# Perceiver layer on one core: the weighted context in four single PSUM banks, with its last sums, the first query products and the down products laid out differently

## The chip, the cores and the metric

The kernel runs on one core of one Trainium2 chip. The metric is device time in microseconds (us) for one execution, lower is better; the figure given is the median of repeated runs. A profile is one further execution recorded by the hardware profiler. All arithmetic is fp32.

A core has five engines that run side by side, each with its own instruction stream: TensorE (PE in the profile; its weight loads appear as PEld), VectorE (DVE), ScalarE (ACT), GpSimd (POOL) and SyncE (SP, which issues most DMA transfers). They hand work to each other through semaphores. TensorE writes its products into PSUM[...].

## The reference

One layer of a Perceiver on 256 tokens x of width 512, with a context c of 25088 rows of width 512:

```python
# 1 cross attention with a sigmoid in place of a softmax
q = layernorm(x) @ Wq.T + bq            # 256 x 128
k = c @ Wk.T + bk                       # 25088 x 128
z = sigmoid(q @ k.T / sqrt(128))        # 256 x 25088
x = x + z @ (c @ Wv.T + bv)
# 2 causal attention: 16 query heads of 64, one shared key and value head
x = x + layernorm(attention(layernorm(layernorm(x))) @ w_out.T)
# 3 experts: a shared one (1024 wide, gated) plus the top 8 of 64 (256 wide each), weighted
h = layernorm(x)
x = x + shared(h) * sigmoid(h @ shared_gate) + sum(w_e * expert_e(h))
```

The kernel uses z @ (c @ Wv.T + bv) = (z @ c) @ Wv.T + rowsum(z) * bv. It keeps two sums over the context: the "weighted context" zc = z @ c (256 x 512) and the "score sums" rowsum(z) (256 values).

## The kernel before, in words

**Context loop (L480-494).** The 25088 rows are taken in 49 groups of 512 (G = 49, four row blocks of 128 each, J = 4). For each group TensorE makes keys (`pk`), scores (`pz`), ScalarE the sigmoid (`zT`), and TensorE adds zT times context to the weighted context (`xacc`). That last product is done by seven block products in place of eight, with sums of blocks made beforehand by VectorE: `query_sums` (S, from zT) and `context_sums` (T, from the context). The seven products (named "00", "01", "2", "3", "1", "4", "11" at L436) are each 128 x 256 and stay in PSUM through all 49 groups. They share banks in pairs: `banks("xacc_0")` and `banks("xacc_1")` are tiles of two banks each. "00" with "01" and "2" with "3" lie in the first tile; "1" with "4", and "11" alone, in the second. VectorE also adds every zT into `zsum` (128 x 4 x 256), from which the score sums come.

**Last sums (L497-546).** After the last group VectorE combines the seven products into zc with eight instructions, TensorE transposes zc in eight blocks (`transposed`, L301), VectorE copies the transposes to zcT, TensorE forms the score sums `pr` from the four parts of zsum, and then py = zcT times Wv for each of the two token tiles (t = 0 and 1). x1, its layernorm `an` and the transposes of an follow.

**Heads (L794-817).** Sixteen heads are handled as eight pairs (NE = 8), which the text calls heads 0 to 7, in a software pipeline. Iteration e transposes the exponentials of head e-2 (`turned`), divides those of head e-1 (`divided`: a reciprocal on VectorE, a product on GpSimd), makes the queries of head e+2 (`queries`: products on TensorE into `pa`, a scaled copy `aq` on VectorE for heads 1 to 3 and on ScalarE for the others), makes the scores of head e (`scored`: products `ps`, mask and maxima on VectorE), the weighted values of head e-2 (`weighted`, `po`), and the exponentials of head e (`exponential`, on ScalarE). When queries run out, parts of the output projection (`fill`, `project`, product `pw`) take their place.

**Experts (L892-1287).** For the shared expert (in four pieces) and eight whole experts: `gate_up` makes `ph` from the tokens and the first weights, ScalarE and VectorE make the hidden values hT, and `down` multiplies them with the second weights for the two token tiles (`pd`), which VectorE weights and adds to `y`. Seven less-used experts are taken in blocks of 32 rows (`few_...`) between them, and `few_spread` adds their result to y.

**Order and buffers.** `in_turn` pins an instruction behind the one traced before it on the same engine; what is not so marked is placed by the scheduler of the framework, which also places all semaphore waits. PSUM is shared out by tags: "one" has three single banks in rotation (`among_three`), "apart" is one bank of its own (`apart`), and "two" has two tiles of two banks (`banks`). `bank(name)` counts its calls: every fourth goes to `apart`, the others to `among_three`. A new tile in a rotation waits until the readers of the one that had its place are done.

```python
        if e == 1:
            queries(e + 1)
        if e != 2 and 0 < e < NE - 2:
            queries(e + 2)
```

These lines (L805-808) stand after the two calls of `divided` and put the queries of heads 2 and 3 there in iteration 1; both go to `apart`.

Of the kernel before, what the change touches and what calls it, by code (L numbers as in the profile page):

```python
# [9 lines left out]
F32 = mybir.dt.float32  # L10
# [4 lines left out]
P = 128  # L15
# [6 lines left out]
def tile_perceiver_layer(  # L22
# [25 lines left out]
    nc = tc.nc  # L48
# [38 lines left out]
    def apart(name):  # L87
        return psum.tile([P, 512], F32, tag="apart", name=name, bufs=1)

    def banks(name):  # L90
        return psum.tile([P, 2, 512], F32, tag="two", name=name, bufs=2)

# [292 lines left out]
    def summed(g, zT):  # L385
# [9 lines left out]

    NP = J // 2
    HD = D // 2
    held = [pair[:, i, :] for pair in (banks("xacc_0"), banks("xacc_1")) for i in range(2)]
    product = {
        nm: held[i // 2][:, (i % 2) * HD : (i % 2 + 1) * HD]  # L400
        for i, nm in enumerate(("00", "01", "2", "3", "1", "4", "11"))
    }
    sums, channel_sums = {}, {}

    def z_of(zT, i, b):

        return zT[:, b::2, i * P : (i + 1) * P]

    def c_of(ct, b, k):
# [22 lines left out]
    def values(g, zT):  # L432
        ct = ctx_tiles.pop(g)
        s1, s2, s3, s4 = sums.pop(g)
        t1, t2, t3, t4 = channel_sums.pop(g)
        for nm, lhs, rhs in (  # L436
            ("00", z_of(zT, 0, 0), c_of(ct, 0, 0)),
            ("01", z_of(zT, 0, 1), c_of(ct, 1, 0)),
            ("2", s2, t2),
            ("3", s3, t3),  # L440
            ("1", s1, t1),
            ("4", s4, c_of(ct, 1, 1)),
            ("11", z_of(zT, 1, 1), t4),
        ):
            for p in range(NP):

                in_turn(
                    nc.tensor.matmul(  # L448
                        product[nm],
                        lhsT=lhs[:, p, :],  # L450
                        rhs=rhs[:, p, :],
                        start=(g == 0 and p == 0 and nm in ("00", "2", "1", "11")),
                        stop=(g == G - 1 and p == NP - 1 and nm in ("01", "3", "4", "11")),
                    )
                )

# [43 lines left out]
    nc.vector.tensor_copy(u2, product["00"])  # L500
# [3 lines left out]
    nc.vector.tensor_add(u4, u2, product["1"])  # L504
    nc.vector.tensor_add(zc[:, 1, HD:D], u3, product["1"])
    nc.vector.tensor_add(zc[:, 0, HD:D], u4, product["4"])
# [5 lines left out]
    for t in range(NT):  # L512
        for j in range(J):
            in_turn(
                nc.tensor.matmul(
                    pr[:, t : t + 1],
                    lhsT=zsum[:, j, t * P : (t + 1) * P],
                    rhs=ones_sb,
                    start=(j == 0),
                    stop=(j == J - 1),  # L520
                )
            )
# [10 lines left out]
    anT = work.tile([P, ND, T], F32, tag="tokT", name="anT")  # L533

    for t in range(NT):
        py = bank(f"py_{t}")
        for c in range(ND):
            in_turn(
                nc.tensor.matmul(
                    py,  # L540
                    lhsT=zcT[:, c, t * P : (t + 1) * P],
                    rhs=wvT_sb[:, c, :],
                    start=(c == 0),
                    stop=(c == ND - 1),
                )
            )
# [5 lines left out]
    cross.close()  # L552

# [62 lines left out]
    def queries(e, lo=0, hi=T):  # L616

        pa = apart(f"pa_{e}_{lo}")
        for c in range(ND):
            in_turn(  # L620
                nc.tensor.matmul(  # L621
                    pa[:, 0 : hi - lo],
                    lhsT=a_wqT_sb[:, c, e * P : (e + 1) * P],
                    rhs=anT[:, c, lo:hi],
                    start=(c == 0),
                    stop=(c == ND - 1),
                )
            )
        to, src = aq[:, e, lo:hi], pa[:, 0 : hi - lo]
        if 0 < e < 4:  # L630
            in_turn(nc.vector.tensor_scalar(to, src, 1.0 / DH, None, ALU.mult))
        else:
            in_turn(nc.scalar.activation(to, src, AF.Copy, scale=1.0 / DH))
# [224 lines left out]
    def route(t):  # L858
        pl = among_three(f"pl_{t}")
        for c in range(ND):  # L860
            in_turn(
                nc.tensor.matmul(
                    pl[:, : E + 1],
                    lhsT=fT[:, c, t * P : (t + 1) * P],
                    rhs=gates_sb[:, c, :],
                    start=(c == 0),
                    stop=(c == ND - 1),
                )
            )
# [70 lines left out]
    def down(n, hT):  # L940
        _, dn = weights.pop(n)
        nm = f"{n[0]}{n[1]}"
        pair = banks(f"pd_{nm}")
        for t in range(NT):
            pd = pair[:, t, :]
            for f in range(NI):
                nc.tensor.matmul(  # L947
                    pd,
                    lhsT=hT[:, f, t * P : (t + 1) * P],
                    rhs=dn[:, f, :],  # L950
                    start=(f == 0),
                    stop=(f == NI - 1),
                )
            w = wsh[:, t, :] if n[0] == "s" else wso[:, t, n[1] : n[1] + 1]
            if n == ("s", 0):
                nc.vector.scalar_tensor_tensor(
                    y[:, t, :], pd, w, x2[:, t, :], ALU.mult, ALU.add
                )
            else:
                nc.vector.scalar_tensor_tensor(  # L960
                    y[:, t, :], pd, w, y[:, t, :], ALU.mult, ALU.add
                )
# [245 lines left out]
        nc.scalar.copy(of_sb[:, r, :], po)  # L1208

    def few_spread():  # L1210
        pair = banks("pd_few")
        for t in range(NT):
            pd = pair[:, t, :]
# [129 lines left out]
```

## Time and profile before

| | us |
|---|---|
| median of 3 runs | 807.11 (806.55 to 807.17) |
| the profiled execution, its own time | 807.09 |
| span in its profile, first to last instruction | 805.2 |
| TensorE busy in the span | 788.5 (98%) |
| VectorE busy | 497.7 (62%) |
| ScalarE busy | 111.5 (14%) |
| GpSimd busy | 19.4 (2%) |
| mean granted TensorE clock | 0.996 of full |

The context loop takes up the span until about 557 us, the last sums and py until 576, the heads until about 630, the output projection and the routing until 649, the experts until 799, and the stores the rest. How to read the lines: the page gives busy time per engine as a share of the span; "chain that ended last" follows the work back from the last instruction. In an answer of the timeline a line is: start, length, engine, line of the kernel, operation, out<-in, shape, how many instructions were merged, and in brackets how long the engine had been idle before and what released it. One matmul of the program is two instructions[...]. The ends of matmuls are modelled, so starts are the surer figures; a releaser is inferred from semaphores.

### The profile page before, as it was taken

What the parts mean: (1) busy time and instruction counts of PE and PEld (TensorE: products, weight loads), DVE (VectorE), ACT (ScalarE), POOL (GpSimd) and SP (SyncE); (2) the same over time, 40 slices, a digit from 0 to 9 for tenths busy, and PEclk for the clock granted to TensorE, in tenths of its full rate; (3) what the DMA queues carried; (4) which work ended last, traced back from release to release, by engine and by line L of the source; (5) the groups of instructions that cost most, each with busy time, mean ns of one, the idle gap of its engine ahead of it and who ended that gap; (6) DMA issues with size and microseconds to landing.
All of it is one profiled execution on the core that took longest, in us unless ns stands there. A gap on an engine that the chain in (4) does not pass through costs nothing.

```text
span 805.2 us, 8713 instructions
## 1 busy us (share of the span) xinstructions
PE 788.5 (98%) x3310; PEld 566.5 (70%) x3310; DVE 497.7 (62%) x822; ACT 111.5 (14%) x246; POOL 19.4 (2%) x42
## 2 busy tenths in 40 slices
PE   9999999999999999999999999999889999999996
PEld 5777777777777777777777777777656586775563
DVE  5766777667776677766777667776446563522222
ACT  2111100111001110011101111011235320110110
POOL 1000000000000000000000000000123000000000
PEclk9999999999999999999999999999999999999999
DMA  9967998999788777887778877710600032489400
GB/s 275 256 162 190 267 252 228 238 248 255 175 195 207 184 180 166 205 201 186 180 174 200 203 185 178 171 49 0 235 2 1 1 129 80 157 319 392 177 1 30
DMA packets 150497, 139.59 MB, mean 173 GB/s; under 512 B 7984, under 2 KB 109872, under 8 KB 150448
## 3 DMA queue, kind: packets, MB, share of 16 engines
q1 hardware_dynamic: 150160, 138.96, 66.7%
q8 instruction: 28, 0.46, 0.2%
q14 instruction: 21, 0.17, 0.1%
q10 hardware_dynamic: 288, 0.00, 0.0%
HBM read 138.42 MB, written 0.52 MB: 173 GB/s over the span
## 4 chain that ended last, share of the span: by engine, by line
PE 94%; DVE 3%; DMA 1%; ACT 1%; POOL 1%; issue 0%; SPq 0%; ACTq 0%; POOLq 0%; DVEq 0%
PE xacc L448 37%; PE pk L347 21%; PE pz L369 11%; PE ph_e L899 7%; PE pd_e L947 3%; PE ph_s L899 3%; PE pa L621 2%; PE pd_s L947 2%; PE ph_few L1169 1%; PE pw L685 1%; PE ps L711 1%; DMA gu_s<-in_s_gate_up 1%; PE pd_few L1215 1%; PE po_few L1200 1%; PE pf L1146 1%; PE ptp L762 1%
## 5 line engine op out<-in xcount | busy, mean ns | idle before, releaser
L347 PE MATMUL pk<-cT,wkT_sb 128*128 128x512 f32 x376 | 169.0, 592 | 0.0
L448 PE MATMUL xacc<-T,S 128*128 128x256 f32 x588 | 134.9, 379 | 0.0
L377 ACT ACTIVATE zT<-pz 128x512 f32<-128x512 f32 x98 | 58.3, 597 | 479.9 <-PE pz L369 479.2
L448 PEld LDWEIGHTS xacc<-T,S 128*128 128x128 f32 x588 | 111.7, 190 | 15.2
L347 PEld LDWEIGHTS pk<-cT,wkT_sb 128*128 128x128 f32 x376 | 71.4, 190 | 69.9 <-issue 67.4
L318 DVE STREAM_TRANSPOSE cT<-quarters 128x2048 f32<-128x2048 f32 x47 | 108.3, 2304 | 0.0
L448 PEld LDWEIGHTS xacc<-ctx,zT 128*128 128x128 f32 x392 | 74.3, 190 | 31.3 <-issue 23.0
L448 PE MATMUL xacc<-ctx,zT 128*128 128x256 f32 x392 | 93.0, 380 | 0.1
L369 PE MATMUL pz<-qT,kT 128*128 128x256 f32 x392 | 92.6, 379 | 0.0
L369 PEld LDWEIGHTS pz<-qT,kT 128*128 128x128 f32 x392 | 74.4, 190 | 10.1
L416 DVE TENSOR_TENSOR S<-zT 128x256 f32<-128x256 f32 x49 | 20.8, 425 | 91.4 <-ACT zT L377 91.4
L356 DVE TENSOR_SCALAR kT<-pk,bk 128x512 f32<-128x512 f32 x49 | 36.8, 751 | 59.8 <-PE pk L347 59.8
L899 PE MATMUL ph_e<-fT,gu 128*128 128x256 f32 x256 | 57.7, 381 | 0.0
L389 DVE TENSOR_TENSOR zsum<-zsum,zT 128x1024 f32<-128x1024 f32 x48 | 56.8, 1184 | 0.0
L899 PEld LDWEIGHTS ph_e<-fT,gu 128*128 128x128 f32 x256 | 47.9, 190 | 11.0 <-issue 3.5
L448 PE MATMUL xacc<-T,zT 128*128 128x256 f32 x196 | 50.3, 379 | 0.0
L448 PE MATMUL xacc<-ctx,S 128*128 128x256 f32 x196 | 50.3, 379 | 0.0
L448 PEld LDWEIGHTS xacc<-T,zT 128*128 128x128 f32 x196 | 37.2, 190 | 5.1
L448 PEld LDWEIGHTS xacc<-ctx,S 128*128 128x128 f32 x196 | 37.2, 190 | 5.1
L427 DVE TENSOR_TENSOR T<-ctx,T 128x512 f32<-128x512 f32 x49 | 33.9, 692 | 1.7
L428 DVE TENSOR_TENSOR T<-ctx 128x512 f32<-128x512 f32 x49 | 33.5, 685 | 0.0
L429 DVE TENSOR_TENSOR T<-T,ctx 128x512 f32<-128x512 f32 x49 | 33.5, 684 | 0.0
(227 smaller groups left out, 616.7 us busy)
## 6 DMA issues: line engine op xcount, KB each, us to landing
ctx<-in_context SPq DMA_DIRECT2D x48, 1024.0 KB, 6.5
quarters<-in_context SPq DMA_DIRECT2D x188, 256.0 KB, 8.4
gu<-in_e_gate_up SPq DMA_DIRECT2D x12, 1024.0 KB, 7.9
dn<-in_e_down SPq DMA_DIRECT2D x11, 512.0 KB, 5.7
gu_s<-in_s_gate_up SPq DMA_DIRECT2D x8, 512.0 KB, 6.0
a_wqT<-in_a_wqT SPq DMA_DIRECT2D x1, 2048.0 KB, 8.5
a_wout<-in_a_woutT SPq DMA_DIRECT2D x1, 2048.0 KB, 8.8
dn_s<-in_s_down SPq DMA_DIRECT2D x4, 512.0 KB, 7.7
```

Of the source, the lines that this page charges most:

```text
L318: in_turn(nc.vector.transpose(cT, q.rearrange("p b (c r) -> p c b r", r=R)))
L347: nc.tensor.matmul(pk, lhsT=w[:, c, :], rhs=cT[:, c, :, :].rearrange("p b r -> p (b r)"), start=(c == 0), stop=(c == ND - 1),)
L356: in_turn(nc.vector.tensor_scalar(kT, pk, bk_sb, None, ALU.add))
L369: nc.tensor.matmul(pz[:, i * T : (i + 1) * T], lhsT=kT[:, j * P : (j + 1) * P], rhs=qT, start=True, stop=True,)
L377: nc.scalar.activation(zT[:, 2 * h : 2 * h + 2, :].rearrange("p j t -> p (j t)"), pz, AF.Sigmoid, scale=1.0 / math.sqrt(QK),)
L389: in_turn(nc.vector.tensor_add(zsum, zsum, zT))
L427: in_turn(nc.vector.tensor_sub(t2, c_of(ct, 1, 1), t1))
L428: in_turn(nc.vector.tensor_sub(t3, c_of(ct, 1, 1), c_of(ct, 0, 1)))
L429: in_turn(nc.vector.tensor_sub(t4, t2, c_of(ct, 1, 0)))
L448: nc.tensor.matmul(product[nm], lhsT=lhs[:, p, :], rhs=rhs[:, p, :], start=(g == 0 and p == 0 and nm in ("00", "2", "1", "11")), stop=(g = ...
L899: nc.tensor.matmul(ph[:, f * T + lo : f * T + hi], lhsT=gu[:, c, col : col + P], rhs=fT[:, c, lo:hi], start=(c == 0), stop=(c == ND - 1),)
L947: nc.tensor.matmul(pd, lhsT=hT[:, f, t * P : (t + 1) * P], rhs=dn[:, f, :], start=(f == 0), stop=(f == NI - 1),)
```

## The change

- The seven products of the weighted context lie in four tiles of one bank each (new pool `pacc`, four buffers) and pair up differently: ("00","01"), ("2","3"), ("1"), ("4","11"). `z_of` exchanges the two token tiles, so each product now stands for the other tile; the last eight sums run in another order and are pinned.
- zc is transposed in four pairs of blocks by the new `turn_zc`, in the order in which the sums end, with the copies of tile 0 on ScalarE and those of tile 1 on VectorE. py takes its four parts in the same order.
- GpSimd adds the four parts of zsum to one, so that `pr` needs one product for each token tile in place of four. `pr` goes to `apart`, py to the three.
- In iteration 1 of the heads, the queries of head 2 come first, ahead of `divided`, and those of head 3 go to the three banks (`where=among_three`).
- The second transposed tile of head 6 is copied by VectorE in place of ScalarE, and one part of the output projection moves ahead of the last transposes.
- The logits of token tile 0 are copied by ScalarE.
- `down` and `few_spread` take a tile of their own for each token tile (the first bank of a two-bank tile, from the pool `pairs`, which is opened where the pool of the context loop is closed) in place of one tile for both.

```diff
+    pacc = cross.enter_context(tc.tile_pool(name="pacc", bufs=4, space=bass.MemoryType.PSUM))
...
-    held = [pair[:, i, :] for pair in (banks("xacc_0"), banks("xacc_1")) for i in range(2)]
-    product = {
-        nm: held[i // 2][:, (i % 2) * HD : (i % 2 + 1) * HD]
-        for i, nm in enumerate(("00", "01", "2", "3", "1", "4", "11"))
-    }
+    product = {}
+    for i, names in enumerate((("00", "01"), ("2", "3"), ("1",), ("4", "11"))):
+        held = pacc.tile([P, 512], F32, tag="acc", name=f"xacc_{i}")
+        for k, nm in enumerate(names):
+            product[nm] = held[:, k * HD : (k + 1) * HD]
...
     def z_of(zT, i, b):
 
+        i = 1 - i
         return zT[:, b::2, i * P : (i + 1) * P]
...
-    nc.vector.tensor_copy(u2, product["00"])
-    nc.vector.tensor_add(zc[:, 0, 0:HD], u2, product["01"])
-    nc.vector.tensor_add(u2, u2, product["2"])
-    nc.vector.tensor_add(u3, u2, product["3"])
-    nc.vector.tensor_add(u4, u2, product["1"])
-    nc.vector.tensor_add(zc[:, 1, HD:D], u3, product["1"])
-    nc.vector.tensor_add(zc[:, 0, HD:D], u4, product["4"])
-    nc.vector.tensor_sub(zc[:, 1, 0:HD], u3, product["11"])
+    for ins in (
+        lambda: nc.vector.tensor_copy(u2, product["00"]),
+        lambda: nc.vector.tensor_add(zc[:, 1, 0:HD], u2, product["01"]),
+        lambda: nc.vector.tensor_add(u2, u2, product["2"]),
+        lambda: nc.vector.tensor_add(u3, u2, product["3"]),
+        lambda: nc.vector.tensor_add(zc[:, 0, HD:D], u3, product["1"]),
+        lambda: nc.vector.tensor_add(u4, u2, product["1"]),
+        lambda: nc.vector.tensor_sub(zc[:, 0, 0:HD], u3, product["11"]),
+        lambda: nc.vector.tensor_add(zc[:, 1, HD:D], u4, product["4"]),
+    ):
+        in_turn(ins())
+
+    nc.gpsimd.tensor_add(zsum[:, 0:2, :], zsum[:, 0:2, :], zsum[:, 2:4, :])
+    nc.gpsimd.tensor_add(zsum[:, 0, :], zsum[:, 0, :], zsum[:, 1, :])
     zcT = work.tile([P, ND, T], F32, tag="tokT", name="zcT")
-    transposed(zcT, zc, "zc")
-
-    pr = bank("pr")
+
+    def turn_zc(t, chunks):
+        lo, hi = chunks[0], chunks[-1] + 1
+        pt = among_three(f"pt_zc_{t}_{lo}")[:, 0 : (hi - lo) * P]
+        for c in chunks:
+            in_turn(
+                nc.tensor.transpose(
+                    pt[:, (c - lo) * P : (c - lo + 1) * P], zc[:, t, c * P : (c + 1) * P], ident
+                )
+            )
+        to = zcT[:, lo:hi, t * P : (t + 1) * P]
+        src = pt.rearrange("p (c q) -> p c q", q=P)
+        if t == 0:
+            in_turn(nc.scalar.copy(to, src))
+        else:
+            in_turn(nc.vector.tensor_copy(to, src))
+
+    turn_zc(0, (2, 3))
+    turn_zc(1, (0, 1))
+    pr = apart("pr")
     for t in range(NT):
-        for j in range(J):
...
+                lhsT=zsum[:, 0, t * P : (t + 1) * P],
...
+    turn_zc(0, (0, 1))
+    turn_zc(1, (2, 3))
...
-        py = bank(f"py_{t}")
-        for c in range(ND):
+        py = among_three(f"py_{t}")
+        order_c = (2, 3, 0, 1)
+        for c in order_c:
...
-            if kt == 0:
+            if kt == 0 or e == NE - 2:
...
+        if e == 1:
+            queries(e + 1)
         if e == 2:
             queries(e + 2)
+        if e == NE + 1:
+            fill(1)
...
         if e == 1:
-            queries(e + 1)
-        if e != 2 and 0 < e < NE - 2:
+            queries(e + 2, where=among_three)
+        elif 2 < e < NE - 2:
             queries(e + 2)
...
-        in_turn(nc.vector.tensor_copy(lg, pl[:, : E + 1]))
+        if t == 0:
+            in_turn(nc.scalar.copy(lg, pl[:, : E + 1]))
+        else:
+            in_turn(nc.vector.tensor_copy(lg, pl[:, : E + 1]))
...
-        pair = banks(f"pd_{nm}")
         for t in range(NT):
-            pd = pair[:, t, :]
+            pd = banks(f"pd_{nm}_{t}")[:, 0, :]
```

`few_spread` changes as `down` does.

More of the change, by code (lines that the diff above doesn't have):

```diff
@@ L88, in apart @@
         return psum.tile([P, 512], F32, tag="apart", name=name, bufs=1)
-    def banks(name):
-        return psum.tile([P, 2, 512], F32, tag="two", name=name, bufs=2)
+    pacc = cross.enter_context(tc.tile_pool(name="pacc", bufs=4, space=bass.MemoryType.PSUM))
     def load(name, shape, src, pool=const):
@@ L451, in values @@
                         rhs=rhs[:, p, :],
-                        start=(g == 0 and p == 0 and nm in ("00", "2", "1", "11")),
-                        stop=(g == G - 1 and p == NP - 1 and nm in ("01", "3", "4", "11")),
+                        start=(g == 0 and p == 0 and nm in ("00", "2", "1", "4")),
+                        stop=(g == G - 1 and p == NP - 1 and nm in ("01", "3", "1", "11")),
                     )
@@ L508, in tile_perceiver_layer @@
+    nc.gpsimd.tensor_add(zsum[:, 0:2, :], zsum[:, 0:2, :], zsum[:, 2:4, :])
+    nc.gpsimd.tensor_add(zsum[:, 0, :], zsum[:, 0, :], zsum[:, 1, :])
     zcT = work.tile([P, ND, T], F32, tag="tokT", name="zcT")
-    transposed(zcT, zc, "zc")
-    pr = bank("pr")
-    for t in range(NT):
-        for j in range(J):
+    def turn_zc(t, chunks):
+        lo, hi = chunks[0], chunks[-1] + 1
+        pt = among_three(f"pt_zc_{t}_{lo}")[:, 0 : (hi - lo) * P]
+        for c in chunks:
             in_turn(
[L515 to L520, printed above, removed]
-                )
-            )
+                nc.tensor.transpose(
+                    pt[:, (c - lo) * P : (c - lo + 1) * P], zc[:, t, c * P : (c + 1) * P], ident
+                )
+            )
+        to = zcT[:, lo:hi, t * P : (t + 1) * P]
[4 more added lines that the diff above has]
+            in_turn(nc.vector.tensor_copy(to, src))
@@ L523, in tile_perceiver_layer @@
+    turn_zc(0, (2, 3))
+    turn_zc(1, (0, 1))
+    pr = apart("pr")
+    for t in range(NT):
+        in_turn(
+            nc.tensor.matmul(
+                pr[:, t : t + 1],
+                lhsT=zsum[:, 0, t * P : (t + 1) * P],
+                rhs=ones_sb,
+                start=True,
+                stop=True,
+            )
+        )
+    turn_zc(0, (0, 1))
+    turn_zc(1, (2, 3))
     rsum = act.tile([P, NT], F32, tag="rsum", name="rsum")
@@ L542, in tile_perceiver_layer @@
                     rhs=wvT_sb[:, c, :],
-                    start=(c == 0),
-                    stop=(c == ND - 1),
+                    start=(c == order_c[0]),
+                    stop=(c == order_c[-1]),
                 )
@@ L552, in tile_perceiver_layer, with banks @@
     cross.close()
+    pairs = ctx.enter_context(tc.tile_pool(name="pairs", bufs=2, space=bass.MemoryType.PSUM))
+    def banks(name):
+        return pairs.tile([P, 2, 512], F32, tag="two", name=name)
     NS = IS // I
@@ L614, in tile_perceiver_layer, with queries @@
     va = hpool.tile([P, NT, DH], F32, tag="va", name="va")
-    def queries(e, lo=0, hi=T):
-        pa = apart(f"pa_{e}_{lo}")
+    def queries(e, lo=0, hi=T, where=apart):
+        pa = where(f"pa_{e}_{lo}")
         for c in range(ND):
@@ L1210, in few_spread @@
     def few_spread():
-        pair = banks("pd_few")
         for t in range(NT):
-            pd = pair[:, t, :]
+            pd = banks(f"pd_few_{t}")[:, 0, :]
             for r in range(NR):
```

## The prediction

> **What bounds the kernel now.** I read the page first (busy shares, the chain that ended last), then busy time by stretch, then the order of time around each edit, then the waits there.
>
> ```profile
> PE 788.5 (98%) x3310; PEld 566.5 (70%) x3310; DVE 497.7 (62%) x822; ACT 111.5 (14%) x246; POOL 19.4 (2%) x42
> PE 94%; DVE 3%; DMA 1%; ACT 1%; POOL 1%; issue 0%; SPq 0%; ACTq 0%; POOLq 0%; DVEq 0%
> ```
>
> TensorE is the bound; other engines carry 6% of the chain. So an edit pays only where TensorE idles, does less, or runs slowly. The stretches say where (columns: stretch, its length, busy us and count of PE, PEld, DVE, ACT, POOL, granted clock, DMA share, GB/s):
>
> ```profile
> 22.00:557.00 535.00, 535.00 (x2106) 399.79 (x2105) 385.10 (x526) 56.08 (x95) 1.45 (x10) 1.00 0.81 192
> 557.00:569.00 12.00, 10.42 (x57) 8.46 (x56) 7.33 (x18) 2.42 (x3) 0.00 (x0) 1.00 0.00 1
> 583.00:598.00 15.00, 12.53 (x65) 9.23 (x65) 6.07 (x15) 2.30 (x11) 1.65 (x2) 0.89 0.02 7
> 598.00:630.00 32.00, 30.32 (x193) 18.02 (x190) 17.95 (x46) 17.47 (x74) 11.56 (x14) 1.00 0.00 1
> 781.00:799.00 18.00, 17.15 (x58) 10.01 (x54) 4.27 (x6) 1.18 (x2) 0.00 (x0) 1.00 0.04 15
> ```
>
> The 49-group loop has no gap. The idle time sits in four places that the diff touches: the last sums (1.58 us), the first heads (2.47 us, with the clock down), the other heads (1.68 us) and the tail (0.85 us). In order of time:
>
> ```profile
> 561.74 0.42 DVE L500 COPY u<-xacc 128x256 f32<-128x256 f32 x1 [0.66 <-PE xacc L448]
> ...
> 564.33 0.42 DVE L504 TENSOR_TENSOR u<-u,xacc 128x256 f32<-128x256 f32 x1 [0.80 <-PE xacc L448]
> ...
> 565.56 0.85 PE L306 MATMUL pt_zc<-ident,zc 128*128 128x128 f32 x6 [1.05 <-DVE zc L506]
> ...
> 566.82 1.95 PE L515 MATMUL pr<-ones_sb,zsum 128*128 128x1 f32 x16 [0.41 <-DVE zcT L309]
> ...
> 590.04 0.40 DVE L631 TENSOR_SCALAR aq<-pa 128x256 f32<-128x256 f32 x1
> 590.50 3.68 PE L621 MATMUL pa<-anT,a_wqT 128*128 128x256 f32 x8 [2.47 <-DVE aq L631]
> ...
> 594.11 0.93 PE L711 MATMUL ps<-kk,aq 64*128 64x128 f32 x8
> ...
> 796.20 0.75 DVE L960 SCALAR_TENSOR_TENSOR y<-pd_e,wso,y 128x512 f32<-128x512 f32 x1 [0.17 <-PE pd_e L947]
> ...
> 797.01 1.98 PE L947 MATMUL pd_e<-dn,hT_e 128*128 128x512 f32 x4 [0.84 <-DVE y L960]
> ```
>
> L500 reads product "00", whose bank was done by 560.0, yet starts at 561.74, when product "3" in the second bank of the same tile ends: a reader waits for the whole two-bank tile. L504 likewise waits for "11". At 797.01 a token tile's down products wait until the other tile's y has been read, though that lies in another bank. At 590.50 the queries wait for a copy on VectorE that had its products at about 588.
>
> [...] after the 2.47 us gap the granted clock is 0.50 from 591 to 594, and the eight query matmuls take 3.68 us, not the 1.9 to 2.0 of the other heads. [...]
>
> **Part 1: last sums, transposes, score sums (L497-546).** TensorE's last xacc step starts at 563.91 (pitch 0.215), so it is free at 564.13 as before. VectorE is free at 561.08 (zsum) and no longer waits for "3": copy 561.1, then dependent steps 0.45 apart, independent ones 0.33: 561.5, 562.0 ("3" done 561.75), 562.4, 562.9 ("1", alone in its bank, done about 562.6), 563.2. Two halves of zc are thus finished by 563.3. The two that need bank ("4","11") start at 564.33 and 564.66 and end at 564.75 and 565.08. Before, three more followed 564.33. TensorE: four transposes of 0.11 from 564.13 to 564.56; two pr products of four instructions at 0.11 in place of sixteen, to 565.0; two transposes from about 565.05; two from 565.27 (565.08 and the 0.15 seen between L506's end and its transpose); py from 565.5. Before: 568.62. **Gain 3.1 us** (12 x 0.11 = 1.3 of it fewer instructions, the rest waits). GpSimd's two adds (1.26 as L678, 0.61 as L748's 128x256) run from 561.2 to 563.2; what hides them is the wait for the xacc products, up to about 564.6. At twice the price they end at 564.9 and cost 0.4; at three times 2.2. A gain of their own is excluded: only pr reads them. ScalarE's two copies (0.39, as L771) fall in a stretch in which it idles until 574; a copy loads no table in this trace (10.42). VectorE's copy of tile 1 ends at about 565.4 and frees the bank that py_0 takes in the ring of three: just in time, 0.1 to 0.3 if late. The shared-expert loads behind pr on SP (568.84 on) start some 3.5 us earlier and are needed at 638.8. The py chain to x1, an and the transposes shifts whole: the chain's "DMA gu_s" before L288 is no cause, since that activation starts 0.04 after its transposes end. Bounds 2.0 to 3.3.
>
> **Part 2: queries (L616, L795-808).** The copy of queries(2) moves ahead of the two reciprocals of head 0, which wait for ScalarE's exponentials (589.05, 589.96); on VectorE it then follows the reduce at 588.1, is 0.42 long and is over before the reciprocal behind it can start at 589.05. queries(3) takes one of three banks and waits for no copy: it follows queries(2) at 587.87, takes 8 x 0.215 and ends at 589.6, and the scores of head 1 start at 589.7 instead of 594.11. **Gain 4.4 us**: 2.6 idle, 1.8 slow clock. What is late next: the second weighted product of head 0, which in the kernel before starts 5.61 after those scores (599.72), behind exponentials (3.1), 1.7 of them, two copies of 0.4. With the same chain it is at 595.3. queries(4) has its bank (copy done 588.6), the transposes have pe (GpSimd done 591.24, wanted 592.4). Bounds: 2.6 if a half-clock window still falls here, 4.7 if the 0.28 extra before the exponentials at 597.42 goes too.
>
> **Part 3: end of the heads (L768, L809).** pT of head 6 goes to VectorE: the weighted product runs unbroken from 624.49 (saves 0.4). The filler put ahead of the last transposes needs oT of that head: 625.3 + 0.1 + 0.38, so it starts at about 625.9, ends at 626.75, past GpSimd's 626.52. Then transposes, two fillers, po at 629.4, and head 7's projection at 630.7, which ends at about 631.6; before, 631.61. **0**, bounds -0.4 to +0.4.
>
> **Part 4: lg of tile 0 to ScalarE (L871).** It waits there behind sd_f (641.64), 0.2 to 0.3 off VectorE, where 0.22 stood beside the wait of the transposes at 642.86. **0.1**, bounds 0 to 0.3.
>
> **Part 5: down products in own tiles (L940, L1210).** The second token tile waits for no y. Tail: 0.84 and 0.1 of refill at 797.01, 0.2 at 792.46, 0.1 in between: **1.3 us**. From 649 to 781 TensorE is busy nearly without a gap, because other matmuls stood between the halves; they come in another order at the same pitch. The first expert's second half (702.58 before) follows its first at about 694.7, so the loads that wait on SP for its weights' place (704.49) go out sooner; nothing on TensorE waited for a load there, so this is 0. The price: two tiles alive instead of two pairs. A tile is free 0.2 + 0.75 + 0.06 = 1.0 after its products, and the other tile's products cover 1.72. Bounds -1 to +2. bank() is called seven times fewer before the experts, so "apart" falls on other products; each bank still comes back after four calls: 0.
>
> **Sum.** 3.1 + 4.4 + 0 + 0.1 + 1.3 = 8.9: the profiled execution's span goes from 805.2 to 796.3, its 807.09 to 798.2. Its own time is at the median, 807.11, so I predict **798.2**. All lower ends together (2.0 + 2.6 - 0.4 + 0 - 1 = 3.2) give 803.9, all upper ones (10.7) 796.4.
>
> **Rivals.** (A, 0.72) As summed, 796.6 to 800.2. (B, 0.16) The queries' gain is half eaten: exponentials of head 1 or a half-clock window take the place of the wait; 798.2 + 2.2 = 800.4, and 802.6 with nothing of it. For: between 598 and 630 only 1.7 us are idle, so lost cover shows at once. Against: the new order has no gap near 2.5 us. (C, 0.03) The changes in the experts' order give it back, 806 to 808. (D, 0.06, slower) The down tiles, now two of one bank, stall TensorE: where VectorE is late, y frees the tile late. For: at 698.99 a y came 4.3 us after its products, behind the seats' comparisons. Priced at the whole 1.0 for each of 13 products (4 shared, 8 experts, the few): 798.2 + 1.3 + 13 = 812.5. It decides from (7.6 + 1.6) / 13 = 0.7 us each. Against: 1.72 covers 1.0, and VectorE is 21% to 50% busy there (5.77 of 28 us, 11.05 of 22). (E, 0.03) Freed order saves in the experts too: 794.5 to 796.6. That the change doesn't do what it says (readers still held by tile) would cost only the tail and part of 1: 800.
>
> **How the numbers follow.** 0.2% is about 1.6 us, what a measurement of this kernel can tell from none. Faster: A, B, E and a little of C, 0.92; same 0.02; slower 0.06. The range 796.0 to 801.5 takes A, half of B, half of E; D is left out. A's own is 796.6 to 800.2.
>
> **What would show it.** pr with 4 instructions and py starting 1.6 us after the last xacc end; query matmuls of head 3 right behind head 2's at 1.9 us and a granted clock of 1.00 after 583; scores of head 1 about 4.5 us after those of head 0; no wait of pd_e for y at the end. Wrong if the 49 groups take another time than 11.2 us each (0.2 us more is 9.8), if pr waits for POOL, or if pd waits for y.

## The result and the profile after

| | before | after |
|---|---|---|
| median of 4 runs each | 807.09 us (806.55 to 807.17) | 798.25 us (798.09 to 798.58) |
| the profiled execution | 807.09 us, span 805.2 | 798.27 us, span 796.4 |
| ratio after/before | | 0.989, 95% interval 0.988 to 0.991 |

The forecast was 798.2 us. The page of the kernel after, its busy shares and the shares of the chain that ended last:

```profile
PE 784.4 (98%) x3298; PEld 564.5 (71%) x3298; DVE 496.6 (62%) x820; ACT 112.3 (14%) x248; POOL 21.4 (3%) x44
...
PE 96%; DVE 2%; ACT 1%; DMA 0%; POOL 0%; issue 0%; ACTq 0%
```

TensorE has twelve instructions less (the score sums) and 96% of the chain instead of 94%. The stretches that answer to those shown of before, at the same stages (same columns: stretch, length, busy us and count of PE, PEld, DVE, ACT, POOL, granted clock, DMA share, GB/s):

```profile
22.00:557.00 535.00, 535.00 (x2106) 399.79 (x2105) 385.02 (x526) 56.16 (x95) 1.47 (x10) 1.00 0.80 192
557.00:566.00 9.00, 8.71 (x45) 6.96 (x44) 6.48 (x16) 2.12 (x5) 2.00 (x2) 1.00 0.00 0
580.00:591.00 11.00, 11.00 (x68) 8.53 (x67) 6.22 (x16) 2.95 (x15) 1.66 (x2) 1.00 0.02 5
590.50:622.50 32.00, 30.86 (x196) 18.48 (x194) 18.41 (x47) 17.10 (x72) 11.58 (x14) 1.00 0.00 1
773.50:791.00 17.50, 16.50 (x49) 8.93 (x47) 5.77 (x8) 0.60 (x1) 0.00 (x0) 1.00 0.04 15
```

The 49 groups take the same time. TensorE's idle time fell from 1.58 to 0.29 us in the last sums, and from 2.47 to nothing in the first heads, where the granted clock is 1.00 throughout (0.89 before). In the other heads it went from 1.68 to 1.14, but that is not a gain of 0.5: a wait of 0.47 us that ends at 623.06 lies just behind the stretch. In the tail TensorE is busy until its last product ends at about 790.0; the missing 1.00 us lies behind that. The order of time of the kernel after, at the places that the prediction shows of before:

```profile
560.94 0.42 DVE L501 COPY u<-xacc 128x256 f32<-128x256 f32 x1
...
564.27 0.42 DVE L507 TENSOR_TENSOR zc<-u,xacc 128x256 f32<-128x256 f32 x1 [0.62 <-PE xacc L448]
...
564.87 0.70 PE L521 MATMUL pt_zc<-ident,zc 128*128 128x128 f32 x4
...
565.32 0.37 ACT L528 COPY zcT<-pt_zc 128x256 f32<-128x256 f32 x1 [0.46 <-PE pt_zc L521]
...
565.75 7.13 PE L564 MATMUL py<-wvT,zcT 128*128 128x512 f32 x16 [0.17 <-ACT zcT L528]
...
583.19 3.72 PE L651 MATMUL pa<-anT,a_wqT 128*128 128x256 f32 x16
...
586.84 0.93 PE L741 MATMUL ps<-kk,aq 64*128 64x128 f32 x8
...
786.41 3.60 PE L983 MATMUL pd_e<-dn,hT_e 128*128 128x512 f32 x8
...
790.04 0.75 DVE L996 SCALAR_TENSOR_TENSOR y<-pd_e,wso,y 128x512 f32<-128x512 f32 x1 [0.97 <-PE pd_e L983]
```

The first sum starts at 560.94 and not 561.74: it no longer waits for the neighbouring bank. The values py start at 565.75 (before 568.62). Both heads' queries run as one piece of sixteen at a granted clock of 1.00, and head 1's scores follow those of head 0 (582.33) after 4.51 us, not 8.93. At 786.41 the last eight down products run without a wait. The gain adds up along the way:

| from the last xacc product's start | before | after | gained |
|---|---|---|---|
| to py | 563.91 to 568.62 | 563.86 to 565.75 | 2.8 |
| from there to the scores of head 0 | 568.62 to 585.18 | 565.75 to 582.33 | 0.0 |
| scores of head 0 to those of head 1 | 585.18 to 594.11 | 582.33 to 586.84 | 4.4 |
| from there to the second half of head 0's weighted product | 594.11 to 599.72 | 586.84 to 592.17 | 0.3 |
| from there to the first expert's hidden products | 599.72 to 685.09 | 592.17 to 677.53 | 0.0 |
| from there to the last y | 685.09 to 799.03 | 677.53 to 790.04 | 1.4 |

### The profile page after: what moved, and what is told of

It is laid out like the page before. It is cut to its first block, busy times and chain, and to the rows that moved or that the text cites. A ratio compares the mean times of both kernels' runs of the same rounds, so it can differ in the third digit from the quotient of the medians.

```text
span 796.4 us, 8701 instructions
## 1 busy us (share of the span) xinstructions
PE 784.4 (98%) x3298; PEld 564.5 (71%) x3298; DVE 496.6 (62%) x820; ACT 112.3 (14%) x248; POOL 21.4 (3%) x44
## 4 chain that ended last, share of the span: by engine, by line
PE 96%; DVE 2%; ACT 1%; DMA 0%; POOL 0%; issue 0%; ACTq 0%
PE xacc L448 37%; PE pk L346 21%; PE pz L368 11%; PE ph_e L936 7%; PE pd_e L983 3%; PE ph_s L936 3%; PE pd_s L983 2%; PE pa L651 2%; PE ph_few L1205 1%; PE pw L715 1%; PE py L564 1%; PE ps L741 1%; PE ptp L792 1%; PE po_few L1236 1%; PE pf L1182 1%; PE pd_few L1250 1%
```

## The experiments

They ran at other times than the comparison above, on three chips, and beside them the kernel before itself falls into groups of runs: 806.7 to 807.2, 808.1 to 808.8 and 809.9 to 810.6 us, with mean clocks of about 0.996, 0.994 and 0.992. The groups are 1.6 to 1.7 us apart, and some variants show them too. What the traces show of these steps stands under pr_four below; they are why variants of the kernel before are compared here by the stretch that was edited, beside their median. The kernel after and all but one of its variants have a single group, and can be held against 798.25 us by their median.

### The queries: order, bank and clock

q_order moves only head 2's queries in the kernel before; q_bank changes only the bank of head 3's; q_warm adds idle work ahead of head 3's; q_undone takes the kernel after and puts both back.

q_order:

```diff
+        if e == 1:
+            queries(e + 1)
...
-        if e == 1:
-            queries(e + 1)
```

q_bank (`queries` gets a parameter `where`, which is `apart` if nothing else is said):

```diff
-        pa = apart(f"pa_{e}_{lo}")
+        pa = where(f"pa_{e}_{lo}")
...
-        if e != 2 and 0 < e < NE - 2:
+            queries(e + 2, where=among_three)
+        elif e != 2 and 0 < e < NE - 2:
             queries(e + 2)
```

q_warm, right ahead of `queries(e + 2)` of iteration 1:

```diff
+            pi = among_three("pi_gap")
+            for _ in range(2):
+                in_turn(
+                    nc.tensor.matmul(
+                        pi, lhsT=a_wqT_sb[:, 0, 0:P], rhs=a_wqT_sb[:, 0, 0:512], start=True, stop=True
+                    )
+                )
```

q_undone:

```diff
-        if e == 1:
-            queries(e + 1)
...
-            queries(e + 2, where=among_three)
-        elif 2 < e < NE - 2:
+            queries(e + 1)
+        if e != 2 and 0 < e < NE - 2:
```

> The kernel before with one edit: head 2's queries go ahead of head 1's scores and probabilities, head 3's stay in the one bank that is kept apart. Theory (the bank decides when head 3's queries start, the order decides what stands ahead of them): head 3's first product waits for the copy of head 2's queries out of that bank, which ends some 0.4 to 0.7 us after head 2's last product; an idle of about 1 us stays[...]. Gain 3.4 to 3.7 us, so 803.4 to 803.7 us. Rival (the order is all of it): the whole 4.4 us, 802.7 us. Rival (the order is worth nothing without the bank): 807.1 us.

> The kernel before with the other edit: head 3's queries go to the three banks in turn, in their old place behind head 1's scores and the division of head 0's probabilities. Theory (the wait for the one bank is what made the idle of 2.47 us, and the idle made the slow clock): both go, gain 4.4 to 4.7 us, so 802.4 to 802.7 us. Rival (the order is needed, since head 3's queries still stand behind a wait): no gain or less than 2 us, 805 to 807.1 us.

> The kernel before with work added and nothing else: two products of 128x512 whose result nobody reads, 0.43 us each at the full clock, right ahead of head 3's queries, so inside TensorE's idle of 2.47 us. Head 3's queries can start no earlier than before. Theory (the idle made the clock fall to half, and the fall made the queries take 3.7 us and not 1.9): the clock stays at 1.0 behind the filler, gain 1.7 to 1.8 us, so 805.3 to 805.4 us. Rival (the queries are slow for another reason, or the idle that is left still halves the clock): 807.1 us.

> The kernel after with this part alone undone: head 2's queries back behind head 1's scores, head 3's back in the bank kept apart. Theory (the part is worth what the two traces show between the two heads' scores, 4.4 us, and 0.28 us more ahead of the second head's weighted values): the idle and the slow clock return, 802.7 to 803.0 us. Rival (its gain overlaps with another part's): less than 4 us lost, under 802 us.

TensorE's order of time in q_order, from the queries of head 2 (589.28) to the scores of head 1; head 0's scores start at 588.43:

```profile
589.28 1.99 PE L621 MATMUL pa<-anT,a_wqT 128*128 128x256 f32 x8
...
591.79 1.99 PE L621 MATMUL pa<-anT,a_wqT 128*128 128x256 f32 x8 [0.52 <-DVE aq L631]
593.72 0.93 PE L711 MATMUL ps<-kk,aq 64*128 64x128 f32 x8
```

The same in q_bank (head 0's scores at 588.44):

```profile
589.30 3.72 PE L621 MATMUL pa<-anT,a_wqT 128*128 128x256 f32 x16
592.95 0.93 PE L711 MATMUL ps<-kk,aq 64*128 64x128 f32 x8
```

In q_warm (head 0's scores at 585.07; pi_gap is the added work):

```profile
587.76 1.88 PE L810 MATMUL pi_gap<-a_wqT 128*128 128x512 f32 x4
...
590.39 1.99 PE L621 MATMUL pa<-anT,a_wqT 128*128 128x256 f32 x8 [0.75 <-DVE aq L631]
592.31 0.93 PE L711 MATMUL ps<-kk,aq 64*128 64x128 f32 x8
```

And in q_undone (head 0's scores at 582.13):

```profile
587.44 3.59 PE L651 MATMUL pa<-anT,a_wqT 128*128 128x256 f32 x8 [2.47 <-DVE aq L661]
590.96 0.93 PE L741 MATMUL ps<-kk,aq 64*128 64x128 f32 x8
```

| | scores of head 0 to head 1 | gain over before's 8.93 | median of the runs |
|---|---|---|---|
| q_order | 5.29 us | 3.6 | 806.05 us (803.01 to 806.96, three groups) |
| q_bank | 4.51 | 4.4 | 804.43 (804.13 to 805.99, two groups) |
| q_warm | 7.24 | 1.7 | 806.97 (805.23 to 808.91, three groups) |
| q_undone | 8.83 | 0.1 | 802.34 (802.25 to 802.71) |

The bank alone is the whole gain, and the rivals that gave the order all of it, or made it a condition, fall. So does the one that gave the order nothing without the bank: alone it is worth 3.6 us. With the old bank and the new order a wait of 0.52 us stays, and the granted clock is 1.00 behind it, from 591 to 595.

The medians mix the groups of runs. The lowest group of q_order, three runs of 803.0 to 803.4, lies just under what was expected, and so does the lowest run of q_warm, 805.23, the only one of its group. No run of q_bank came down to its 802.4 to 802.7: its groups, 804.1 to 804.5 and 805.9 to 806.0, lie one step of 1.7 us and two steps above, and in its profiled execution (805.89) the clock is at 0.50 for 6.83 us right behind the score sums.

q_warm separates the two halves of the gain. In it the queries wait for the same copy as before and start no earlier; but with 1.88 us of work in the gap they take 1.99 us instead of 3.68. So the slow clock here followed from the gap and was worth 1.7 us by itself (1.00 with the gap filled, 0.50 without), and the wait is the other 2.7. The stretch that holds the queries, in the kernel before and, in the fence below it, in q_warm (columns as above):

```profile
591.00:593.00 2.00, 2.00 (x6) 1.64 (x5) 0.00 (x0) 0.00 (x0) 0.24 (x1) 0.50 0.03 8
```

```profile
591.00:593.00 2.00, 2.00 (x15) 1.40 (x13) 0.42 (x1) 0.00 (x0) 0.13 (x1) 1.00 0.04 8
```

TensorE reads as busy for 2.00 of 2.00 us in both; only the number of instructions (6 against 15) and the clock tell them apart.

Undone alone in the kernel after, the part costs 4.1 us by the medians, 4.3 by the stretch: less than the 4.4 to 4.7 that were expected. The 0.3 us ahead of the second weighted product, which the prediction had put at this part's upper end, stay there in q_undone (1.41 us from the start of head 0's weighted product to the transposes behind it, as in the kernel after; before, 1.69) and are missing in q_bank (1.72). So they do not come from the queries. They lie in front of head 1's exponentials, in the kernel before and, in the fence below it, in the kernel after:

```profile
597.42 0.37 ACT L736 ACTIVATE pe<-ps,nmx 128x128 f32<-128x128 f32 x1 [7.49 <-PE ptp L762]
```

```profile
589.86 0.37 ACT L766 ACTIVATE pe<-ps,nmx 128x128 f32<-128x128 f32 x1 [2.79 <-DVE nmx L755]
```

In the kernel before and its three variants, the first exponential is released by head 0's transposes, 3.3 us after head 1's scores started. In the kernel after it is released by VectorE's maxima, after 3.0 us, and so it is in every variant of that kernel, those included that take one part back. What made the difference stays open.

### The last sums: single banks, and who sums the scores

acc_pairs, in the kernel after:

```diff
-    pacc = cross.enter_context(tc.tile_pool(name="pacc", bufs=4, space=bass.MemoryType.PSUM))
+    pacc = cross.enter_context(tc.tile_pool(name="pacc", bufs=2, space=bass.MemoryType.PSUM))
...
-        held = pacc.tile([P, 512], F32, tag="acc", name=f"xacc_{i}")
+        if i % 2 == 0:
+            two = pacc.tile([P, 2, 512], F32, tag="acc", name=f"xacc_{i // 2}")
...
-            product[nm] = held[:, k * HD : (k + 1) * HD]
+            product[nm] = two[:, i % 2, k * HD : (k + 1) * HD]
```

pr_four, in the kernel after:

```diff
-    nc.gpsimd.tensor_add(zsum[:, 0:2, :], zsum[:, 0:2, :], zsum[:, 2:4, :])
-    nc.gpsimd.tensor_add(zsum[:, 0, :], zsum[:, 0, :], zsum[:, 1, :])
...
-                lhsT=zsum[:, 0, t * P : (t + 1) * P],
+                    lhsT=zsum[:, j, t * P : (t + 1) * P],
...
+                    start=(j == 0),
+                    stop=(j == J - 1),
```

> The kernel after with the four accumulators in two tiles of two banks, as before, and the new order of the sums kept. Theory (a reader waits for all of its tile, not for its bank): VectorE's first copy waits for the products of bank 1 too, and its reader of bank 2 for those of bank 3; 0.7 to 1.0 us lost, 799.0 to 799.3 us. Rival (a reader waits for its bank alone): 798.3 us.

> The kernel after with GpSimd's two sums of score columns taken out again: pr is made from the four parts by 16 matmul instructions and not 4. Theory (these stand on TensorE ahead of the last transposes, on the path from the last sum to the end): 12 instructions more at the 0.10 to 0.13 us that four of them take in the trace, 1.2 to 1.5 us lost, 799.5 to 799.8 us. Rival (they fit into the wait for VectorE's last sums): 798.3 us.

acc_pairs took 799.24 us (798.84 to 799.44), 1.0 more than the kernel after, as the theory said. Its order of time:

```profile
561.67 0.43 DVE L502 COPY u<-xacc 128x256 f32<-128x256 f32 x1 [0.66 <-PE xacc L449]
...
566.47 1.55 PE L565 MATMUL py<-wvT,zcT 128*128 128x512 f32 x3 [0.24 <-ACT zcT L529]
```

The copy is back where the kernel before had it (561.74), with the same wait of 0.66 us for products it doesn't read, and py starts 0.7 us later than at 565.75. That lag of 0.72 us is unchanged at the last y (790.76 against 790.04), so 0.7 is what the banks are worth; the rest of what the profiled execution (799.44) has more lies in the stores behind the last y (6.9 us to the end of the span, against 6.4). So the readers of these accumulators wait for the tile: here 0.66 us for products that lie in its other bank.

pr_four has two groups, 799.22 to 799.43 us and 801.01 to 801.21. The lower one, two runs, is 1.1 us above the kernel after: the price of the twelve instructions (expected 1.2 to 1.5). The profiled execution is of the upper group; in it py starts at 567.10, with the granted clock still at 1.00 (564 to 566; 0.97 from 566 to 568), 1.35 us later than in the kernel after. Its score sums, in order of time:

```profile
564.51 1.84 PE L536 MATMUL pr<-ones_sb,zsum 128*128 128x1 f32 x16
```

and the stretches from there on:

```profile
564.00:566.00 2.00, 2.00 (x21) 1.93 (x19) 1.08 (x3) 0.37 (x1) 0.00 (x0) 1.00 0.03 8
566.00:568.00 2.00, 1.76 (x10) 1.10 (x10) 0.99 (x3) 1.31 (x2) 0.00 (x0) 0.97 0.15 25
568.00:570.00 2.00, 2.00 (x4) 0.72 (x3) 0.91 (x2) 0.35 (x1) 0.00 (x0) 0.50 1.05 356
```

The granted clock falls to 0.50 here too, though TensorE shows only 0.24 us without work in four. In the traces a slow stretch inside the kernel lasts 3.41 us, or twice that: 3.41 in the kernel before, in q_undone and here, 6.83 in the profiled executions of q_order and q_bank, whose score sums are those of the kernel before. Half of 3.41 is 1.7 us of lost work, the distance between the groups, and 1.7 of 805 us takes 0.002 off the mean clock, as from group to group.

What sets a slow stretch off was shown at one place only: in the heads it follows a gap of 2.47 us, and with 1.88 us of work in that gap it did not come (q_warm). Around pr_four's score sums TensorE had by its busy time hardly idled, 0.24 us in four, and the clock fell all the same. So busy time alone does not tell where it falls: the sixteen instructions of one column each look like 1.84 us of work. Why the stretch comes in some runs and not in others was not shown.

The kernel after, with four instructions of one column and not sixteen, and its variants other than pr_four show a single group each, in 46 runs together. In the comparison the kernel before was not slow there either (its profile has 1.00 from 562 to 590, and its four runs are one group), so this adds nothing to the 8.8 us; beside the experiments it does. No run of the kernel before from an upper group was profiled: that the same stretch makes its groups is argued from q_order and q_bank and from the mean clocks.

### The down products

down_pairs, in the kernel after:

```diff
+        pair = banks(f"pd_{nm}")
...
-            pd = banks(f"pd_{nm}_{t}")[:, 0, :]
+            pd = pair[:, t, :]
```

down_one, in the kernel after:

```diff
+    pd_only = banks("pd_only")[:, 0, :]
...
-            pd = banks(f"pd_{nm}_{t}")[:, 0, :]
+            pd = pd_only
```

In both, pd_few is treated likewise.

> The kernel after with the down products laid as before: the two halves of an expert share one tile of two banks. Theory (the reader of half 0 waits for the products of half 1, and the next product waits for both, as the two traces show at the first expert and at the end): 1.3 us lost, 799.5 to 799.6 us. Rival (that gain came from the stages ahead and only showed here): 798.3 us.

> The kernel after with all down products in one single bank, so that each product of 512 columns waits for the reader of the one before it. This prices the stall that the forecast's case of a slower kernel assumed (1.0 us at each of 13 products, deciding at 0.7 us each). If that price holds: 13 us lost, about 811 us. Theory (TensorE has other products in its order between two down products, so the bank is mostly free again in time): 1 to 3 us lost, 799.5 to 801.5 us.

down_pairs took 800.64 us (800.55 to 800.74): 2.4 us lost, not 1.3. Both places, in order of time:

```profile
688.62 0.30 PE L1175 MATMUL pt_share<-ident,share 128*128 128x128 f32 x1 [0.79 <-DVE share L1159]
...
790.59 1.98 PE L984 MATMUL pd_e<-dn,hT_e 128*128 128x512 f32 x4 [0.84 <-DVE y L997]
```

The wait at the end is that of the kernel before. The one at 688.62 is in neither of the two kernels: here three transposes of the shares (tile `share`) stand together, and the third waits for VectorE. In the kernel before other matmuls stand between them (from 695.14 on), in the kernel after the second half's products (from 687.31 on). By the traces 1.1 us are lost up to the second expert's down products and 1.4 behind them. The second figure is what the change removed (1.3 in the comparison); the first is the price of an order that is not the old one.

down_one took 807.20 us (807.02 to 807.64), 8.9 us lost: far beyond the 1 to 3 that the theory gave it, and below the 13 of the other case. Its order of time near the end:

```profile
784.18 1.98 PE L984 MATMUL pd_only<-dn,hT_e 128*128 128x512 f32 x4 [0.84 <-DVE y L997]
786.20 0.75 DVE L997 SCALAR_TENSOR_TENSOR y<-pd_only,wso,y 128x512 f32<-128x512 f32 x1 [2.08 <-PE pd_only L984]
787.01 2.84 PE L1251 MATMUL pd_only<-of_sb,shareT 128*128 128x512 f32 x6 [0.85 <-DVE y L997]
```

From 784.18 to 787.01 are 2.83 us, of which four instructions at their pitch of 0.43 (from start to start) fill 1.72: 1.1 us lost where two products meet. TensorE waits 0.78 to 0.85 us for y at seven such meetings, up to 7.7 us together, and the 0.8 of the first expert (a wait as in down_pairs) make nearly all of the 8.9. So the forecast's rival D had the right price per stall (1.0), but a place where it does not arise: it takes a single tile, and even then it comes seven times and not thirteen. With two alive, the kernel after has no wait of this kind.

### The end of the heads, and two further steps

heads_undone, in the kernel after:

```diff
-            if kt == 0 or e == NE - 2:
+            if kt == 0:
...
-        if e == NE + 1:
-            fill(1)
...
-        if t == 0:
-            in_turn(nc.scalar.copy(lg, pl[:, : E + 1]))
-        else:
-            in_turn(nc.vector.tensor_copy(lg, pl[:, : E + 1]))
+        in_turn(nc.vector.tensor_copy(lg, pl[:, : E + 1]))
```

further, in the kernel after (`later` is the old tile of zcT; part_py issues py's products for the parts named; x1 is written only later, so half of it can hold a part; py of tile 1 goes to `apart`):

```diff
...
-        to = zcT[:, lo:hi, t * P : (t + 1) * P]
+        if t == 1:
+            to = later[:, lo:hi, P:T]
+        elif lo == 0:
+            to = x1[:, 1, 0:T].rearrange("p (c q) -> p c q", q=P)
+        else:
+            to = work.tile([P, 2, P], F32, tag="zcT_2", name="zcT_2", bufs=1)
...
+    py_0 = among_three("py_0")
+    part_py(py_0, 0, (2, 3))
     turn_zc(0, (0, 1))
...
-    fillers = [(0, e) for e in range(NE - 1)] + [(1, 0), (1, 1)]
+    fillers = [(0, e) for e in range(NE - 2)] + [(1, 0), (0, NE - 2), (1, 1)]
...
-            fill(2)
+            fill(2 if e < NE + 1 else 1)
```

split_only has the three tiles of further and nothing else of it: py and the fillers stand as in the kernel after. best is split_only with the fillers of further.

> The kernel after with two parts undone: at the end of the heads ScalarE makes both copies of the last head's probabilities but one and the filling products stand as before, and the first half's router logits are copied by VectorE again. Theory (both parts move work that something else hides, as the equal differences between the two traces at these places show): 798.0 to 798.5 us. Rival (each hides 0.3 to 0.5 us): up to 799.0 us.

> The kernel after, taken two steps further. First, the transposed sums lie in three tiles and not one, so that the first two products of half 0's values wait for the first copy of ScalarE alone and stand ahead of the last transposes: 0.2 to 0.4 us gained, if a wait goes by the whole tile. Second, one filling product of half 1 changes places with one of half 0 at the end of the heads, and one is kept for the last head's copy: of the waits of 0.47 and 0.47 us there, 0.3 to 0.8 us gained. Theory: 797.0 to 797.8 us. Rival (the waits only move to the next copy): 798.3 us.

> The kernel after with the transposed sums in three tiles and not one, and every instruction in its place. Theory (the values' first weight load, which reads the half that ScalarE copied first, waits for ScalarE's second copy because both lie in one tile): in tiles of their own the values start right behind the last transpose, and the wait of 0.17 us in the trace is gone; 0.15 to 0.25 us gained, 798.0 to 798.1 us, and in the trace the first of the values starts before the second copy of ScalarE has ended. Rival (that load has to wait for this copy in any case): 798.25 us, and the values start behind the copy.

> Both steps that the runs so far support together: the transposed sums in three tiles with the order of the kernel after, and the new places of the filling products at the end of the heads. The version before it, with the first products of the values ahead of the last transposes, measured 797.3 us and gained 0.84 us at the end of the heads and nothing at the values. If the two add: 0.15 to 0.25 us below that, 797.05 to 797.2 us. Rival (no gain at the values): 797.3 to 797.4 us.

heads_undone took 798.22 us (798.08 to 798.33): Parts 3 and 4 of the prediction are worth nothing together that these runs can tell. further took 797.31 us (797.25 to 797.43), inside what was expected, but not as expected. In the kernel after the projection waits twice for a copy of oT:

```profile
618.29 1.13 PE L715 MATMUL pw<-a_wout,oT 128*128 128x512 f32 x2 [0.47 <-ACT oT L820]
...
623.06 5.42 PE L715 MATMUL pw<-a_wout,oT 128*128 128x512 f32 x12 [0.47 <-ACT oT L820]
```

In further it waits for none:

```profile
617.87 1.12 PE L727 MATMUL pw<-a_wout,oT 128*128 128x512 f32 x2
...
621.50 6.28 PE L727 MATMUL pw<-a_wout,oT 128*128 128x512 f32 x14
```

There lies the gain: from the scores of head 0 to the first expert's hidden products it takes 94.36 us, the kernel after 95.20. At the values there is none. Their first half starts early, but it now delays the transposes, and the second half waits for those:

```profile
564.94 1.98 PE L557 MATMUL py<-wvT,zcT 128*128 128x512 f32 x4
...
566.76 0.60 PE L523 MATMUL pt_zc<-ident,zc 128*128 128x128 f32 x4
...
567.61 1.98 PE L557 MATMUL py<-wvT,x 128*128 128x512 f32 x4 [0.24 <-ACT x L536]
```

split_only (798.16 us, 798.10 to 798.42) shows that the tile is not to blame either. Its products read a tile that ScalarE's first copy alone wrote, and yet:

```profile
565.38 0.37 ACT L536 COPY x<-pt_zc 128x256 f32<-128x256 f32 x1 [0.46 <-PE pt_zc L523]
...
565.80 1.98 PE L557 MATMUL py<-wvT,zcT 128*128 128x512 f32 x4 [0.17 <-ACT x L536]
```

The wait of 0.17 us for the second copy is unchanged, so the theory falls and its rival holds. The compiled order has py's first product wait for ScalarE alone and not for VectorE. That fits an accumulator in the bank of the transposes that ScalarE copied last, and not in that of VectorE's first copy, as the prediction had it. This is argued; no run moved py to another bank by itself, and a wait that the compiled program places ahead of all of py's products would look the same. best took 797.25 us (797.22 to 797.44), the same as further: the new places of the fillers carry it, and with 1.0 us less than the kernel after (0.9 less than split_only, on the same chip) it beats both kernels; its ratio to the kernel before on that chip, some of whose runs have the slow stretch, is 0.986, 95% interval 0.984 to 0.989.

## Why the prediction was right

The time was met to 0.1 us, and the terms one by one nearly so, by the mechanisms that the prediction named. That it is 0.1 and not 0.3 is luck: 0.3 us missing in one part were made up by 0.3 us from another place.

- **Part 1** gave 3.1 and measured 2.8. Its last sums, transposes and score sums came within 0.2 us of the times written down, GpSimd's included (561.11 to 563.19, against 561.2 to 563.2; its first add took 1.27 us beside VectorE's sums, 1.26 at L678). The mis-sized term is the last: "py from 565.5" was 565.75. "ScalarE's two copies fall in a stretch in which it idles" was true, but the second one ends at 565.69 and is what py waits for; 0.25 us. The bank of py_0, named there as the one that VectorE's copy frees, was probably the wrong one. Two pieces of the part were shown alone, at the start of py: single banks 0.7 (acc_pairs), GpSimd's sums 1.35 (pr_four; 12 x 0.11 = 1.3 was written down). If the two add, the rest, about 0.8, is the new order of sums and copies, which no run undid.
- **Part 2** gave 4.4 and measured 4.4: 2.7 for the wait and 1.7 for the clock (q_warm; 2.6 and 1.8 were written down). Its order of the instructions was credited along with the bank; q_bank shows that the bank is enough, q_order that the order alone would have brought 3.6.
- **0.3 us ahead of the second weighted product** lay outside the sum, as an upper end of Part 2. They came, at the place that it named (before head 1's exponentials), but not through the queries; they made up for the 0.3 missing in Part 1.
- **Parts 3 and 4**, 0 and 0.1, measured 0.0 (heads_undone, and equal differences between the two traces on both sides of them).
- **Part 5** gave 1.3 and measured 1.4, of which 1.3 lie behind the second expert's first down products: the last ones ran without the wait for y. The four amounts written down for it add to 1.24, so the 1.3 is rounded up. The experts' order, which rival C feared, changed nothing else.
- **Rivals.** B had no place: in the kernel after the granted clock is 1.00 from 583 to 599. D's price was right and its condition absent. E and C did not occur. Readers "held by tile" are real (0.66 us in acc_pairs), and there the change does take its effect by separating the tiles.

Of what the prediction said would show it, four instructions of pr, the sixteen query products in one piece, a clock of 1.00, 4.5 us between the scores and the absent wait of pd_e are in the lines above; py came 1.9 us after the last xacc product's start. The 1.6 of the prediction is by its own times (563.91 to 565.5) counted from that start too, though it says "end".

## What to carry to other kernels

Look at the granted clock as well as the busy time: here it was at 0.50 for 3.41 us behind a gap of 2.47 us, which cost 1.7 us beside the gap while the matmuls read as fully busy, and it was at 0.50 for 3.41 or 6.83 us at sixteen products of one column or right behind them, in some runs and not in others. One wait for a copy out of the only bank of its kind cost 4.4 us in all, and another bank removed it without any change in the order. When several waits stand near each other, name for each copy who waits for it, also on an engine that is idle: the 0.25 us missed here hung on ScalarE, which was 14% busy. And take back each part of a change alone: one of them (down_pairs) cost more going back than it had brought.

## What the runs showed that was not expected

- The slow clock has a second place, the score sums and transposes behind the last group, where TensorE idles 1.05 and 0.41 us and then runs sixteen instructions of one column. It comes in some runs and not in others, in steps of 1.6 to 1.7 us: beside the experiments the kernel before had, by its times, 0, 1 or 2 steps (806.7 to 810.6 us), pr_four 0 or 1. The slow stretches are 3.41 us long, or 6.83.
- Filling a gap of 2.47 us with 1.88 us of work that nobody reads made the kernel before 1.7 us shorter at that place.
